# A skip term put into the PSUM bank ahead of the products of a Mamba-2 chunk

## The chip, the cores and the metric

The kernel runs on one NeuronCore of a Trainium2 chip, all in fp32. The metric is the device time of one execution in microseconds; the time of the kernel before is the median of three runs. One further execution was profiled, and every duration below is from that one.

## What is computed

The input is one sequence of 2048 tokens and 1024 channels. It is layer-normalised, and the output is the input plus two branches of the normalised `xn`: a Mamba-2 mixer (64 heads of 64 channels in 8 groups, state size 128), and a dense layer with a mixture of eight low-rank adapters. Of the mixer, this is what matters here:

```python
xBC = silu(conv(hbc))                        # four taps along the tokens
state = state * dA_t + dtx_t * B_t           # for each token t
y_t   = state . C_t
y  = y + x * D                               # the skip: one D per head
yg = y.reshape(L, 8, 512)                    # eight groups of 512 channels
yn = yg * rsqrt(mean(yg * yg) + eps) * norm_weight
out = (yn * silu(gate)) @ out_proj_w.T
```

## The kernel before

Everything is kept with channels on the partitions and tokens along the free dimension. The large products (input projection, base layer, output projection) are done by Strassen-Winograd schemes: seven products in place of eight, with sums formed on VectorE and GpSimd. Over the first 2700 us or so the input projection and the scan run interleaved, and the output projection follows.

**The stream of products.** `pair` makes seven products of one pair of weight tiles, each of four matmuls with 512 moving columns (eight records in the trace, for a fp32 matmul is issued as two instructions). It is a generator, and `products(n, side)` takes n products from it and puts the steps of `side` between them. A product's bank comes from the pool `ps_proj` (four banks). Its sums are taken out by VectorE (L478, L482, and L531 in `stored`) or by ScalarE (L474, L529), and for the gate ScalarE then applies Silu (L533).

**The scan.** The sequence is cut into two segments of 1024 tokens, a segment into eight groups and two halves of 512: 32 blocks. A block has four chunks of 128 tokens, and each chunk has a slot in the main loop, some 128 slots in all. In a slot the loop issues, in this order: one product; `norm_mean` of the block before (first slot only); `scan_b` of this chunk; the first step of `scan_a` for the next chunk (the decay scan, L688); a product; the second step of `scan_a`; two products; its third step; and what products are left. The convolution of the next block (`conv`, L640, L646, L653) is spread over the second and third slots of a block, `norm_squares` over the fourth slot, and `norm_gate` over the first slot of the next block.

- `scan_a`, second step: one product C.B and a transpose of B into the bank `aux` (`ps_cb`), copied out by ScalarE as `cbm` (L698) and `bt` (L700); VectorE then multiplies the decays by `cbm` (L702). Third step: four transposes of x into `aux` (`ps_xt`), and sixteen ScalarE copies with a scale: `xdt` (L713) and `xdd` (L721).
- `scan_b`: for each of eight heads a product of `xdt` with the decayed C.B, 128 tokens wide and 64 output partitions, into the bank `y` of the pool `ps_one` (`ps_y`); four products of the state with C into the bank `e` (`ps_e`); on VectorE `ecp * ps_e` (L763) and the sum with `ps_y` into the SBUF tile `y` (L764), or a plain copy (L761) where there is no state yet; then the new state in the bank `st` (L766 to L778).
- `norm_squares`: for each of four tiles, `x * D + y` on VectorE, written over x (L797); squares of it on ScalarE, written over `y` (L802); two sums on VectorE (L804, L805). `norm_mean` adds over channels on TensorE (`ps_nv`, in the bank `aux`) and takes the root on ScalarE (L813).

Each pool `ps_one` bank has one buffer, so whoever writes it next waits until its last reader is done. TensorE's instructions, and the scaled copies of `scan_a`, keep the order of the program (`keep_in_program_order`); the order of the other instructions in each engine's queue is chosen by the framework when it builds the kernel, and is then fixed. Each engine takes its queue in order.

Of the kernel before, what the change touches and what calls it, by code (L numbers as in the profile page):

```python
# [8 lines left out]
F32 = mybir.dt.float32  # L9
AF = mybir.ActivationFunctionType  # L10
ALU = mybir.AluOpType
# [16 lines left out]
P = 128  # L28
TS = 1024
NS = L // TS  # L30
TB = 512
Q = 128
# [10 lines left out]
def mamba_lora_kernel(  # L43
# [17 lines left out]
    nc = tc.nc  # L61
# [9 lines left out]
    ps_one = ctx.enter_context(tc.tile_pool(name="ps_one", bufs=1, space=bass.MemoryType.PSUM))  # L71
    scan_ctx = ExitStack()
    p1 = scan_ctx.enter_context(tc.tile_pool(name="p1", bufs=1))
# [4 lines left out]
    def mm(*args, **kw):  # L78
        tc.keep_in_program_order(nc.tensor.matmul(*args, **kw))  # L79

    def gp(s, *args):

        ins = nc.gpsimd.tensor_tensor(*args)  # L83
        if s:
            tc.keep_in_program_order(ins)

    def transpose(out, in_):
        tc.keep_in_program_order(nc.tensor.transpose(out, in_, ident))  # L88
# [4 lines left out]
    ident = const.tile([P, P], F32, name="ident")  # L93
# [45 lines left out]
    dsk = p1.tile([P, INNER // P], F32, name="dsk")  # L139
# [465 lines left out]
    def steps(gen, n):  # L605

        return [lambda: next(gen, None) for _ in range(n)]


    xbc_of = {}  # L610
# [46 lines left out]
    mid_of = {}  # L657
    decay_of = {}

    def load_decays(s, g, half, c):  # L660

        da_d, run_d = decay_d[s, half * NQ + c]
        n = f"{s}_{g}_{half}_{c}"
        dab = p2.tile([P, HG * Q], F32, tag="dab", name=f"dab_{n}")
        nc.sync.dma_start(
            dab,
            da_d[g * HG : (g + 1) * HG, :].rearrange("h t -> (h t)").unsqueeze(0)
            .to_broadcast([P, HG * Q]),
        )
        ecp = p2.tile([P, 4, Q], F32, tag="ecp", name=f"ecp_{n}")  # L670
        runs = run_d[g * HG : (g + 1) * HG, :].rearrange("(j a) t -> a j t", a=2)
        for a in range(2):
            nc.sync.dma_start(
                ecp[a * HP : (a + 1) * HP],
                runs[a].unsqueeze(0).to_broadcast([HP, 4, Q]),
            )
        decay_of[s, g, half, c] = dab.rearrange("p (h t) -> p h t", t=Q), ecp

    def scan_a(s, g, half, c):

        key = s, g, half, c
        n = f"{s}_{g}_{half}_{c}"
        dab, ecp = decay_of.pop(key)
        hs = slice(g * HG, (g + 1) * HG)
        cs = slice(c * Q, (c + 1) * Q)

        es = p1.tile([P, HG, Q], F32, tag="es", name=f"es_{n}")
        nc.vector.tensor_tensor_scan(  # L688
            es.rearrange("p h t -> p (h t)"), dab.rearrange("p h t -> p (h t)"), here, 0.0,
            ALU.mult, ALU.add,  # L690
        )
        yield
        xg, bc = xbc_of[s, g, half]
        psm = ps_one.tile([P, 2, Q], F32, tag="aux", name=f"ps_cb_{n}")
        mm(psm[:, 0, :], bc[:, 0, cs], bc[:, 1, cs], start=True, stop=True)
        transpose(psm[:, 1, :], bc[:, 0, cs])
        cbm = p2.tile([P, Q], F32, tag="cbm", name=f"cbm_{n}")
        nc.scalar.copy(cbm, psm[:, 0, :])  # L698
        bt = p2.tile([P, Q], F32, tag="bt", name=f"bt_{n}")
        nc.scalar.copy(bt, psm[:, 1, :])  # L700
        ms = dab
        nc.vector.tensor_tensor(  # L702
            ms, es, cbm.unsqueeze(1).to_broadcast([P, HG, Q]), ALU.mult
        )
        yield
        pst = ps_one.tile([P, 4, Q], F32, tag="aux", name=f"ps_xt_{n}")
        for j in range(4):
            transpose(pst[:, j, :], xg[:, j, cs])
        xdt = p2.tile([P, HG, HP], F32, tag="xdt", name=f"xdt_{n}")
        x_t = pst.rearrange("p j (a q) -> p (j a) q", q=HP)  # L710
        for h in range(HG):
            at = g * HG + h
            ins = nc.scalar.activation(  # L713
                xdt[:, h, :], x_t[:, h, :], AF.Copy,
                scale=dt_of[s][:, half * NQ + c, at : at + 1],
            )
            tc.keep_in_program_order(ins)

        xdd = p1.tile([P, HG, HP], F32, tag="xdd", name=f"xdd_{n}")
        for h in range(HG):  # L720
            ins = nc.scalar.activation(  # L721
                xdd[:, h, :], xdt[:, h, :], AF.Copy, scale=es[:, h, Q - 1 : Q]
            )
            tc.keep_in_program_order(ins)
        mid_of[key] = ms, ecp, bt, xdt, xdd
        yield

    y_of = {}
    state_of = {}

    def scan_b(s, g, half, c):
        xg, bc = xbc_of[s, g, half]
        ms, ecp, bt, xdt, xdd = mid_of.pop((s, g, half, c))
        n = f"{s}_{g}_{half}_{c}"
        hs = slice(g * HG, (g + 1) * HG)
        cs = slice(c * Q, (c + 1) * Q)
        begins, ends = half == 0 and c == 0, half == 1 and c == NQ - 1
        first = s == 0 and begins
        last = s == NS - 1 and ends
        if c == 0:  # L740
            y_of[s, g, half] = p1.tile([P, 4, TB], F32, tag="y", name=f"y_{n}")
        if begins:
            state_of[g] = p2.tile([P, HG * HP], F32, tag="state", name=f"state_{s}_{g}")
            if s:
                nc.sync.dma_start(state_of[g], kept["state", g])
        sv = state_of[g]
        y = y_of[s, g, half]
        psy = ps_one.tile([P, 4, Q], F32, tag="y", name=f"ps_y_{n}")
        pse = None if first else ps_one.tile([P, 4, Q], F32, tag="e", name=f"ps_e_{n}")
        for h in range(HG):  # L750
            a, j = h % 2, h // 2
            o = slice(a * HP, (a + 1) * HP)
            mm(psy[o, j, :], xdt[:, h, :], ms[:, h, :], start=True, stop=True)
        if not first:
            for j in range(4):
                mm(
                    pse[:, j, :], sv[:, j * P : (j + 1) * P], bc[:, 1, cs],
                    start=True, stop=True,
                )
        if first:  # L760
            nc.vector.tensor_copy(y[:, :, cs], psy)  # L761
        else:
            nc.vector.tensor_tensor(ecp, ecp, pse, ALU.mult)  # L763
            nc.vector.tensor_tensor(y[:, :, cs], ecp, psy, ALU.add)  # L764
        if last:
            return  # L766
        pss = ps_one.tile([P, HG * HP], F32, tag="st", name=f"ps_st_{n}")
        mm(pss, bt, xdd.rearrange("p h q -> p (h q)"), start=True, stop=True)
        if first:
            nc.scalar.copy(sv, pss)  # L770
        else:
            s3 = sv.rearrange("p (h q) -> p h q", q=HP)
            gp(
                s, s3, s3,
                tot_of[s][:, half * NQ + c, hs].unsqueeze(2).to_broadcast([P, HG, HP]),
                ALU.mult,
            )
            nc.vector.tensor_tensor(sv, sv, pss, ALU.add)  # L778
        if ends:
            kept["state", g] = dram.tile([P, HG * HP], F32, tag=f"st_{g}", name=f"st_{g}")  # L780
            nc.sync.dma_start(kept["state", g], sv)
# [10 lines left out]

    def norm_squares(s, g, half):

        y, xg = y_of[s, g, half], xbc_of[s, g, half][0]
        for j in range(4):
            nc.vector.scalar_tensor_tensor(  # L797
                xg[:, j, :], xg[:, j, :], dsk[:, 4 * g + j : 4 * g + j + 1], y[:, j, :],
                ALU.mult, ALU.add,
            )  # L800
            if j % 2:
                nc.scalar.activation(y[:, j - 1 : j + 1, :], xg[:, j - 1 : j + 1, :], AF.Square)  # L802
                yield
        nc.vector.tensor_tensor(y[:, 0:2, :], y[:, 0:2, :], y[:, 2:4, :], ALU.add)  # L804
        nc.vector.tensor_tensor(y[:, 0, :], y[:, 0, :], y[:, 1, :], ALU.add)  # L805
        yield
# [90 lines left out]
    here = p1.tile([P, HG * Q], F32, name="here")  # L897
# [58 lines left out]
    load_decays(*blocks[0], 0)  # L956
    products(14, steps(conv(*blocks[0]), 7))
    load_decays(*blocks[0], 1)
    for _ in scan_a(*blocks[0], 0):
        pass  # L960
    done = 7 * PRE
# [16 lines left out]
    for b, blk in enumerate(blocks):  # L978
        s, g, half = blk
# [15 lines left out]
        for c in range(NQ):  # L995
            slot += 1
            n = target(slot) - done
# [30 lines left out]
            if c == 0 and prev:  # L1028
                norm_mean(*prev)
            scan_b(*blk, c)  # L1030
            if b == 14 and c:
                next(left_sums)
# [31 lines left out]
            if after == 0 and c == 3:  # L1064
                sm = lp.tile([P, 2, NSM], F32, tag="sm", name=f"sm_{piece[0]}_{piece[1]}")
                ps = ps_one.tile([P, 2, NSM], F32, tag="st", name=f"ps_sm_{piece[1]}")
# [40 lines left out]
    for _ in passes[1:]:  # L1107
        o = places[-1]
# [125 lines left out]
    for t, (s, p) in enumerate(passes):  # L1234
        last = t + 1 == len(passes)
        for u, i in enumerate(units):
# [89 lines left out]
            for n, j in enumerate(inner):  # L1326
                w = w_ready.pop(0)
                ps = {1: pa, 2: pa, 6: px, 7: px, 4: px, 5: py, 3: py}[j]
                for q in range(2):
                    for k in range(KH):  # L1330
                        mm(
                            ps[:, q, :], w[:, q, k, :], ops[j][:, k, :],
                            start=(n < 3 and q + k == 0), stop=(k == KH - 1), skip_group_check=True,
# [69 lines left out]
```

## Time and profile before

| what | value |
|---|---|
| median of three runs | 3449.89 us (3449.82 to 3451.58) |
| the profiled execution | 3453.59 us, of it 3451.8 us from the first to the last instruction |
| TensorE busy | 3409.2 us (99%), 12818 matmul instructions |
| VectorE busy | 2501.2 us (72%), 2861 instructions |
| ScalarE busy | 1164.7 us (34%), 3182 instructions |
| GpSimd busy | 696.1 us (20%), 443 instructions |
| mean granted TensorE clock | 0.997 |

The page gives busy time by engine, the chain of work that ended last, and groups of instructions by line; "L797" is line 797 of the kernel before, and `xg<-xg,dsk,y` is what is written and what is read. Matmuls all have line 79 (the helper `mm`) or 88 (`transpose`), so they are told apart by the tile. A matmul's duration in the trace overlaps with the next one's: a product of eight records takes 3.43 us from its start to the next one's. In the time line, "x8" merges equal neighbours, and what stands in brackets is the idle time before and what ended it.

### The profile page before, as it was taken

What the parts mean: (1) busy time and instruction counts of PE and PEld (TensorE: products, weight loads), DVE (VectorE), ACT (ScalarE), POOL (GpSimd) and SP (SyncE); (2) the same over time, 40 slices, a digit from 0 to 9 for tenths busy, and PEclk for the clock granted to TensorE, in tenths of its full rate; (3) what the DMA queues carried; (4) which work ended last, traced back from release to release, by engine and by line L of the source; (5) the groups of instructions that cost most, each with busy time, mean ns of one, the idle gap of its engine ahead of it and who ended that gap; (6) DMA issues with size and microseconds to landing.
All of it is one profiled execution on the core that took longest, in us unless ns stands there. A gap on an engine that the chain in (4) does not pass through costs nothing.

```text
span 3451.8 us, 38274 instructions
## 1 busy us (share of the span) xinstructions
PE 3409.2 (99%) x12818; PEld 1992.3 (58%) x12818; DVE 2501.2 (72%) x2861; ACT 1164.7 (34%) x3182; POOL 696.1 (20%) x443
## 2 busy tenths in 40 slices
PE   9999999999999999999999999999999999999999
PEld 7444544544545544454455445444444588888888
DVE  7548877877977877777787877777775466566665
ACT  2234453444444443444445444444442100000000
POOL 3122223222222211322223232222321000000000
PEclk9999999999999999999999999999999999999999
DMA  6546655655666676887778887777778687586654
GB/s 235 186 166 197 205 191 186 211 187 197 203 200 204 205 254 219 291 256 231 236 242 260 236 258 244 245 237 236 228 239 267 243 277 242 196 299 188 214 164 146
DMA packets 530324, 769.83 MB, mean 223 GB/s; under 512 B 35152, under 2 KB 264656, under 8 KB 527440
## 3 DMA queue, kind: packets, MB, share of 16 engines
q1 hardware_dynamic: 530128, 767.39, 68.7%
q8 instruction: 102, 1.67, 0.2%
q14 instruction: 94, 0.77, 0.1%
HBM read 516.64 MB, written 250.61 MB: 222 GB/s over the span
## 4 chain that ended last, share of the span: by engine, by line
PE 84%; DVE 9%; issue 3%; ACT 2%; DMA 1%; POOL 0%; SPq 0%; DVEq 0%; ACTq 0%; POOLq 0%
PE ps_x_x L79 12%; PE ps_x_w L79 8%; PE ps_a_x L79 8%; PE ps_y_x L79 8%; PE ps_x_g L79 7%; PE ps_a_w L79 6%; PE ps_y_w L79 6%; PE ps_y_g L79 5%; PE ps_a_g L79 4%; PE ps_y L79 3%; PE ps_e L79 3%; PE ps_st L79 2%; PE ps_x_b L79 2%; DVE xg L646 2%; PE ps_a_b L79 2%
## 5 line engine op out<-in xcount | busy, mean ns | idle before, releaser
L83 POOL TENSOR_TENSOR state<-state,tot 128x512 f32<-128x512 f32 x112 | 153.7, 1373 | 1326.0 <-PE ps_e L79 1199.8
L688 DVE TENSOR_TENSOR_SCAN es<-dab,here 128x1024 f32<-128x1024 f32 x128 | 304.6, 2380 | 83.4 <-ACT xdd L721 81.8
L646 DVE SCALAR_TENSOR_TENSOR xg<-rawx,cw,xg 128x512 f32<-128x512 f32 x384 | 339.2, 933 | 18.7 <-ACT xg L640 18.0
L79 PE MATMUL ps_x_w<-t,w 128*128 128x256 f32 x1344 | 303.8, 379 | 0.0
L713 ACT ACTIVATE xdt<-ps_xt,dt 128x64 f32<-128x64 f32 x1024 | 223.8, 333 | 209.7 <-PE ps_xt L88 209.7
L79 PEld LDWEIGHTS ps_x_w<-t,w 128*128 128x128 f32 x1344 | 255.4, 190 | 41.5 <-issue 7.7
L721 ACT ACTIVATE xdd<-xdt,es 128x64 f32<-128x64 f32 x1024 | 261.9, 388 | 0.0
L1340 ACT COPY s<-ps_a_w 128x512 f32<-128x512 f32 x28 | 16.4, 586 | 636.0 <-PE ps_a_w L79 555.5
L83 POOL TENSOR_TENSOR wo<-wo 128x512 f32<-128x512 f32 (+1 forms) x112 | 213.4, 1906 | 6.8
L79 PE MATMUL ps_a_w<-q,w 128*128 128x256 f32 x896 | 202.5, 379 | 0.0
L702 DVE TENSOR_TENSOR dab<-es,cbm 128x1024 f32<-128x1024 f32 x128 | 180.1, 1407 | 29.6 <-ACT cbm L698 29.6
L79 PEld LDWEIGHTS ps_a_w<-q,w 128*128 128x128 f32 x896 | 170.2, 190 | 23.6 <-issue 0.5
L79 PEld LDWEIGHTS ps_y<-dab,xdt 128*64 128x64 f32 x2048 | 114.6, 139 | 105.1 <-ACT xdd L721 38.7
L79 PE MATMUL ps_x_x<-op_again,s_x 128*128 128x512 f32 x384 | 172.7, 592 | 0.0
L79 PE MATMUL ps_y_x<-op_again,s_x 128*128 128x512 f32 x384 | 172.7, 592 | 0.0
L79 PE MATMUL ps_a_x<-op_again,a_x 128*128 128x512 f32 x384 | 172.7, 592 | 0.0
L79 PE MATMUL ps_x_x<-op,s_x 128*128 128x512 f32 x368 | 165.5, 592 | 0.0
L79 PE MATMUL ps_y_x<-op,s_x 128*128 128x512 f32 x368 | 165.5, 592 | 0.0
L79 PE MATMUL ps_a_x<-op,a_x 128*128 128x512 f32 x368 | 165.4, 592 | 0.0
L79 PE MATMUL ps_y<-dab,xdt 128*64 128x128 f32 x2048 | 146.6, 284 | 7.8 <-ACT xdt L713 7.8
L531 DVE TENSOR_TENSOR ev<-ps_x_x,s_x 128x512 f32<-128x512 f32 x94 | 64.5, 687 | 120.5 <-PE ps_x_x L79 116.1
L646 DVE SCALAR_TENSOR_TENSOR bc<-rawb,cw,bc 128x512 f32<-128x512 f32 x192 | 145.7, 790 | 1.9 <-ACT bc L640 1.0
(236 smaller groups left out, 6118.6 us busy)
## 6 DMA issues: line engine op xcount, KB each, us to landing
w<-w SPq DMA_DIRECT2D x196, 512.0 KB, 3.7
dab<-da_d SPq DMA_DIRECT2D x128, 512.0 KB, 5.5
raw<-ev SPq DMA_DIRECT2D x192, 256.0 KB, 3.3
a_x<-in_w_in_dram SPq DMA_DIRECT2D x168, 256.0 KB, 4.2
w<-wo SPq DMA_DIRECT2D x96, 448.0 KB, 4.3
ecp<-run_d SPq DMA_DIRECT2D x256, 128.0 KB, 4.0
gate<-ev SPq DMA_DIRECT2D x128, 256.0 KB, 3.9
sg<-gate SPq DMA_DIRECT2D x32, 1024.0 KB, 7.8
```

Source lines behind the costliest of these rows:

```text
L79: tc.keep_in_program_order(nc.tensor.matmul(*args, **kw))
L83: ins = nc.gpsimd.tensor_tensor(*args)
L531: nc.vector.tensor_tensor(e, ps, add, alu)
L646: nc.vector.scalar_tensor_tensor(dst[:, i, :], raw[:, i, k : k + TB], cw[:, ti, k : k + 1], dst[:, i, :], ALU.mult, ALU.add,)
L688: nc.vector.tensor_tensor_scan(es.rearrange("p h t -> p (h t)"), dab.rearrange("p h t -> p (h t)"), here, 0.0, ALU.mult, ALU.add,)
L702: nc.vector.tensor_tensor(ms, es, cbm.unsqueeze(1).to_broadcast([P, HG, Q]), ALU.mult)
L713: ins = nc.scalar.activation(xdt[:, h, :], x_t[:, h, :], AF.Copy, scale=dt_of[s][:, half * NQ + c, at : at + 1],)
L721: ins = nc.scalar.activation(xdd[:, h, :], xdt[:, h, :], AF.Copy, scale=es[:, h, Q - 1 : Q])
L1340: nc.scalar.copy(s1, pa)
```

## The change

The skip term is no longer added by VectorE after the scan. For each chunk ScalarE writes `x * D` of its 128 tokens into the bank `y`, in four instructions, and the eight products of `scan_b` then add to what lies there (`start=False`). `scan_a` takes the bank, in its second step, after the copies `cbm` and `bt`; before, `scan_b` took it. The one VectorE sum that reads the bank (L764, or the copy L761) now gives the finished value and writes it over x. The four `x * D + y` of a block are gone, and the tile `y` now only holds the squares. Ahead of the first chunk one matmul with 512 columns is added, that writes the bank with `start=True`[...].

```diff
@@ scan_a, second step, after the copies cbm and bt
+        psy = ps_one.tile([P, 4, Q], F32, tag="y", name=f"ps_y_{n}")
+        for j in range(4):
+            at = 4 * g + j
+            nc.scalar.activation(
+                psy[:, j, :], xg[:, j, cs], AF.Copy, scale=dsk[:, at : at + 1]
+            )
@@ scan_b
-        if c == 0:
-            y_of[s, g, half] = p1.tile([P, 4, TB], F32, tag="y", name=f"y_{n}")
...
-        psy = ps_one.tile([P, 4, Q], F32, tag="y", name=f"ps_y_{n}")
...
-            mm(psy[o, j, :], xdt[:, h, :], ms[:, h, :], start=True, stop=True)
+            mm(
+                psy[o, j, :], xdt[:, h, :], ms[:, h, :], start=False, stop=True,
+                skip_group_check=True,
+            )
...
         if first:
-            nc.vector.tensor_copy(y[:, :, cs], psy)
+            nc.vector.tensor_copy(xg[:, :, cs], psy)
         else:
             nc.vector.tensor_tensor(ecp, ecp, pse, ALU.mult)
-            nc.vector.tensor_tensor(y[:, :, cs], ecp, psy, ALU.add)
+            nc.vector.tensor_tensor(xg[:, :, cs], ecp, psy, ALU.add)
@@ norm_squares
-        y, xg = y_of[s, g, half], xbc_of[s, g, half][0]
-        for j in range(4):
-            nc.vector.scalar_tensor_tensor(
-                xg[:, j, :], xg[:, j, :], dsk[:, 4 * g + j : 4 * g + j + 1], y[:, j, :],
-                ALU.mult, ALU.add,
-            )
-            if j % 2:
-                nc.scalar.activation(y[:, j - 1 : j + 1, :], xg[:, j - 1 : j + 1, :], AF.Square)
-                yield
+        xg = xbc_of[s, g, half][0]
+        y = y_of[s, g, half] = p1.tile([P, 4, TB], F32, tag="y", name=f"sq_{s}_{g}_{half}")
+        for j in (0, 2):
+            nc.scalar.activation(y[:, j : j + 2, :], xg[:, j : j + 2, :], AF.Square)
+            yield
@@ ahead of the first chunk
+    ps = ps_one.tile([P, 4 * Q], F32, tag="y", name="ps_clear")
+    mm(ps, ident, here[:, 0 : 4 * Q], start=True, stop=True)
```

More of the change, by code (lines that the diff above doesn't have):

```diff
@@ L724, in scan_a @@
             tc.keep_in_program_order(ins)
-        mid_of[key] = ms, ecp, bt, xdt, xdd
+        mid_of[key] = ms, ecp, bt, xdt, xdd, psy
         yield
@@ L732, in scan_b @@
         xg, bc = xbc_of[s, g, half]
-        ms, ecp, bt, xdt, xdd = mid_of.pop((s, g, half, c))
+        ms, ecp, bt, xdt, xdd, psy = mid_of.pop((s, g, half, c))
         n = f"{s}_{g}_{half}_{c}"
@@ L746, in scan_b @@
         sv = state_of[g]
-        y = y_of[s, g, half]
-        psy = ps_one.tile([P, 4, Q], F32, tag="y", name=f"ps_y_{n}")
         pse = None if first else ps_one.tile([P, 4, Q], F32, tag="e", name=f"ps_e_{n}")
```

## The prediction

> **What bounds the kernel now.** I read the busy times first, then the chain, then the gaps of TensorE one by one, then what lies around each.
>
> ```profile
> span 3451.8 us, 38274 instructions
> PE 3409.2 (99%) x12818; PEld 1992.3 (58%) x12818; DVE 2501.2 (72%) x2861; ACT 1164.7 (34%) x3182; POOL 696.1 (20%) x443
> PE 84%; DVE 9%; issue 3%; ACT 2%; DMA 1%; POOL 0%; SPq 0%; DVEq 0%; ACTq 0%; POOLq 0%
> ```
>
> TensorE is the bound. It idles 3451.8 - 3409.2 = 42.6 us, some 9 of them at the very start and end (4.4 before the first matmul, about 4.9 after the last). The chain's 9% for VectorE is no 300 us to be had: where TensorE waits 2 us, the chain goes back through all the VectorE work that made it late. What the change can win is the idle time that is VectorE's doing, and no more. So: who makes TensorE wait?
>
> ```profile
> PE ps_nv L79 <- ACT xdt L713: 10.5, 4, 3.3
> PE ps_y L79 <- ACT xdt L713: 7.8, 5, 4.6
> PE ps_x_x L79 <- DVE ev L531: 2.8, 3, 1.3
> PE ps_x_g L79 <- DVE ev L531: 2.5, 5, 0.9
> ```
>
> (Columns: us in total, times, longest.) The first row names ScalarE's `xdt`, but ScalarE is 34% busy. The time line of one of the four, engine by engine, shows what held it:
>
> ```profile
> 1557.20 5.42 DVE L797 SCALAR_TENSOR_TENSOR xg<-xg,dsk,y 128x512 f32<-128x512 f32 x4
> ...
> 1566.68 3.52 DVE L646 SCALAR_TENSOR_TENSOR bc<-rawb,cw,bc 128x512 f32<-128x512 f32 x5
> 1570.11 0.68 DVE L531 TENSOR_TENSOR ev<-ps_x_g,s_g 128x512 f32<-128x512 f32 x1
> ```
> ```profile
> 1570.83 0.63 ACT L533 ACTIVATE ev<-ev 128x512 f32<-128x512 f32 x1 [6.46 <-DVE ev L531]
> 1571.37 1.73 ACT L713 ACTIVATE xdt<-ps_xt,dt 128x64 f32<-128x64 f32 x8
> ```
> ```profile
> 1573.15 1.12 PE L79 MATMUL ps_nv<-y,ones 128*128 128x512 f32 x2 [3.27 <-ACT xdt L713]
> ```
>
> VectorE runs without a pause from L797 to L531; ScalarE's Silu (L533) waits for L531, `xdt` stands behind it in ScalarE's queue, and TensorE waits for `xdt`. The four skip sums took 5.42 us here.
>
> [...] For `xdd` (64 columns, pointer scale) [...] the trace has eight in 2.04 us with the last lasting 0.388, so 236 ns. [...] no trace of before shows an engine-written seed. [...]
>
> **The change, part by part.**
>
> *VectorE, removed.*
>
> ```profile
> L797 DVE SCALAR_TENSOR_TENSOR xg<-xg,dsk,y 128x512 f32<-128x512 f32 x128 | 119.6, 990 | 0.0
> ACT y L802 <- DVE xg L797: 109.9, 43, 8.6
> ```
>
> 119.6 us of VectorE work go, 3.7 us per block (990 ns on average, 745 in the median; the long ones run beside GpSimd's sums). Most of it lay beside running products and is worth nothing. I went through every gap of TensorE. Those with an L797 in the backlog of VectorE that made it: 0.26 at 1417, 3.27 at 1570, 0.28 and 2.10 at 2158 and 2166, 0.37 and 2.45 at 2314 and 2318, 2.69 at 2469: 11.4 us. Three were followed by a slower clock: from `ps_nv` to the next product took 5.54, 5.52 and 5.52 us, and 3.94 after the gap at 2318 where the clock stayed up, so 1.6 us each, 4.8 us: 16.2 us in all. Three more gaps, at 701, 951 and 1199, end the router's long chain of small VectorE steps. VectorE works without a pause from L797 up to them, but the chain's first step (L311) needs ScalarE's copy of the router sums, which ended 0.86, 0.20 and 0.62 us before it began; more than that can't be won: **1.7 us**. What is late next: at 1570, VectorE 5.4 us earlier puts L531 at about 1566.7 (then bound by its own product and five `bc` steps), Silu ends at 1567.4, `xdt` at about 1569.5, and TensorE comes at 1569.9. So that gap closes with 0.4 us to spare; the three others have more. The other gaps stay: 4.58 us at 447 plus 1.8 of clock (9% of 20 us) come from the same chain, but there VectorE paused for 1.2 us between L797 and it; two of 0.9 at 726 and 1224 wait for ScalarE's copy of the decays; 0.5 to 1.3 us at 1607, 1973, 2126, 2349 and 2506 come from the `xg` convolution in the third slot.
>
> *ScalarE, added.* Four writes of 128 columns per chunk. [...] from the narrower price of `cbm` (261 ns, the next starting 160 ns later) 0.75 us. I take 1.3[...]. Where do they lie? Behind `bt`, with ScalarE idle until the transposes come; this row alone is 210 us:
>
> ```profile
> ACT xdt L713 <- PE ps_xt L88: 209.7, 48, 6.9
> L764 DVE TENSOR_TENSOR y<-ecp,ps_y 128x512 f32<-128x512 f32 x120 | 80.9, 674 | 2.2
> ```
>
> Cost 0. If that cover is gone in a slot, `xdt` is 1.3 us later, and TensorE has a product of 3.4 us between `ps_xt` and what needs `xdt`.
>
> *The new wait.* ScalarE's first write waits until L764 (or L761) of the chunk before has read the bank. I compared the end of all 120 L764 with the end of the `bt` that follows: L764 is done earlier in 116 (median 3.0 us earlier); in four it is later, by 0.16, 0.35, 0.93 and 2.14 us, and there `xdt` starts 4.8 to 14 us after it. Behind the waiting write stand the evacuations L474/L529, Silu and `xdt`; all come later than that. Cost 0, at worst 2 us in one slot.
>
> *TensorE.* `ps_y` already waits for `xdt`, which stands behind the writes in ScalarE's queue, so it gets no later wait. Adding in place of overwriting: a fp32 matmul is two records, [...] and both go at the same pace (16 in 1.02 us). Cost 0. The clearing matmul: two records of 512 columns at 0.43 us, **0.9 us**, on the bound, as nothing hides it. The square waits for L764 in place of L797, so comes earlier. No DMA is added or moved.
>
> *Sum.* 16.2 + 1.7 - 0.9 = 17.0 us off the profiled 3453.6 us: 3436.6. That execution was 3.7 us above the median, so against the median: 3449.9 - 17.0 = 3432.9, say 3433.
>
> **The rivals.**
>
> *A larger gain.* The queues' orders are made anew, and a lighter VectorE might also let the gaps of the `xg` convolution (4.4 us) and the one at 447 (6.4 with its clock) go. For it: VectorE is 72% busy and late by 1 us or less in most of them. Against it: L797 isn't in the slots concerned. With 9 of those us: 3424. Chance 0.16.
>
> *Given back by the order.* The writes aren't kept in program order, and on ScalarE they are ready before `cbm`. Or a step slips in front of an evacuation elsewhere, and new gaps of 1 to 3 us come in some five to eight slots: 13 us back, 3446. Nothing in the profile shows the new order, so I give it 0.19.
>
> *Slower.* The writes stand ahead of `cbm` in ScalarE's queue. Then `cbm` comes up to 1.3 us later, VectorE stands still before L702 for as long, and in the third slot of each block, where five gaps show that VectorE has no slack, the evacuations behind it make TensorE wait. 31 such slots x 1.3 = 40 us, less 17: 3473. It decides where L764 ends less than 1.3 us before `ps_cb` is ready. Against it: in those slots L764 ended 1.9, 2.1 and 3.0 us ahead of `cbm` (2117, 1598, 2343), though only 0.6 at 1969. [...] Chance 0.09.
>
> *It doesn't do what it says*: if products overwrote the seed, times would be those of the forecast; no case of its own.
>
> **How the numbers follow.** The forecast, 3433 (3427 to 3440), has 0.56, the larger gain 0.16, given back 0.19, slower 0.09. A measurement of this kernel can tell about 0.2%, or 7 us: faster means under 3443, slower over 3456.8. Faster: 0.56 + 0.16 + a fifth of "given back" = 0.75; slower 0.09 and a little of "given back", 0.10; the same 0.15. The range leaves out the slower case and the far ends of the two next: 3419 to 3449.
>
> **What would show it.** Right: no row of L797; gaps of `ps_nv` behind `xdt` gone, or under 1 us in all; clock 1.00 around them; L802 waiting little; the gap at 447 still there; `ps_y` at 1.02 us per chunk; the four writes at about 1.3 us behind `bt`, ended ahead of `xdt`. Wrong: TensorE idle still over 35 us, new gaps with `cbm` or the writes behind them, `ps_y` slower than 1.02 us per chunk.

## The result, and the profile after

The kernel after takes 3439.63 us (median of six, 3437.45 to 3442.42) against 3451.36 (six, 3449.82 to 3453.5) for the kernel before: a ratio of 0.9965, with a 95% interval of 0.9952 to 0.9978, so 12 us off, between 8 and 17. The two profiled executions lie 16.1 us apart (3453.59 and 3437.5), with spans of 3451.8 and 3435.7. They flatter the change: a gap of TensorE at 141 us, ahead of the scan, cost 3.1 us less after (the gap itself 3.97 against 1.99, the rest in the product behind it, which took 6.34 us before and 5.21 after where the next ones take 3.43; the granted clock in the 20 us behind the gap was 0.86 and 0.91). In the profiles of the experiments below it is between 2.4 and 4.1 us whatever the edit.

The page's busy times and the engines' shares of the chain, after:

```profile
span 3435.7 us, 38674 instructions
PE 3404.6 (99%) x12820; PEld 1989.8 (58%) x12820; DVE 2410.5 (70%) x2733; ACT 1338.9 (39%) x3694; POOL 697.2 (20%) x443
PE 87%; DVE 8%; issue 2%; DMA 2%; ACT 2%; SPq 0%; DVEq 0%; ACTq 0%
```

TensorE idles 31.1 us, where it idled 42.6. It is also busy 4.6 us less, in spite of the clearing matmul, since fewer of its matmuls run at the slow clock: in the 20 us after the gaps at 1570, 2166 and 2469 the granted clock was 0.91, and at the same three places of the run after it is 1.00. Idle time fell by 11.5 and busy time by 4.6, together 16.1. The waits of TensorE in the kernel after (us in total, times, longest) say which idle time went:

```profile
PE ps_y L79 <- ACT xdt L720: 6.9, 5, 4.6
...
PE ps_x_x L79 <- DVE ev L531: 4.1, 4, 1.3
PE ps_x_g L79 <- DVE ev L531: 3.3, 6, 1.1
...
PE ps_nv L79 <- ACT xdt L720: 0.6, 1, 0.6
```

The row of `ps_nv` fell from 10.5 to 0.6 us; the two rows behind L531 grew from 5.3 to 7.4. The same slot that the prediction took apart (product, `ps_nv`, `xdt`), now about 5 us earlier in the run, on VectorE, ScalarE and TensorE:

```profile
1554.72 4.78 DVE L646 SCALAR_TENSOR_TENSOR bc<-rawb,cw,bc 128x512 f32<-128x512 f32 x3
...
1562.90 2.19 DVE L646 SCALAR_TENSOR_TENSOR bc<-rawb,cw,bc 128x512 f32<-128x512 f32 x3
1565.01 0.68 DVE L531 TENSOR_TENSOR ev<-ps_x_g,s_g 128x512 f32<-128x512 f32 x1
```
```profile
1556.15 1.56 ACT L705 ACTIVATE ps_y<-xg,dsk 128x128 f32<-128x128 f32 x4
1557.65 0.26 ACT L698 COPY cbm<-ps_cb 128x128 f32<-128x128 f32 x1
...
1565.72 0.63 ACT L533 ACTIVATE ev<-ev 128x512 f32<-128x512 f32 x1 [4.99 <-DVE ev L531]
1566.26 1.73 ACT L720 ACTIVATE xdt<-ps_xt,dt 128x64 f32<-128x64 f32 x8
```
```profile
1563.81 3.60 PE L79 MATMUL ps_y_g<-op_again,s_g 128*128 128x512 f32 x8
1568.04 1.12 PE L79 MATMUL ps_nv<-sq,ones 128*128 128x512 f32 x2 [0.63 <-ACT xdt L720]
```

L531 starts 1.2 us after the start of the last product ahead of `ps_nv` (1563.81), where it was 3.8 us before. The gap is 0.63, from 3.27. It isn't quite closed because three convolution steps moved into the place of L797 and took 1.59 us each there, 4.78 together; the three further down take 0.73 each. And the writes stand ahead of `cbm`, not behind `bt`.

Two groups of the page before, and three of the page after (busy us, mean ns of one | idle before it, and who ended that):

```profile
L702 DVE TENSOR_TENSOR dab<-es,cbm 128x1024 f32<-128x1024 f32 x128 | 180.1, 1407 | 29.6 <-ACT cbm L698 29.6
L646 DVE SCALAR_TENSOR_TENSOR bc<-rawb,cw,bc 128x512 f32<-128x512 f32 x192 | 145.7, 790 | 1.9 <-ACT bc L640 1.0
```

```profile
L705 ACT ACTIVATE ps_y<-xg,dsk 128x128 f32<-128x128 f32 x512 | 190.2, 371 | 222.5 <-DVE xg L770 192.9
L709 DVE TENSOR_TENSOR dab<-es,cbm 128x1024 f32<-128x1024 f32 x128 | 177.6, 1388 | 39.3 <-ACT cbm L698 39.0
L646 DVE SCALAR_TENSOR_TENSOR bc<-rawb,cw,bc 128x512 f32<-128x512 f32 x192 | 163.8, 885 | 1.9 <-ACT bc L640 1.3
```

L709 is the former L702. The `bc` steps rose from 145.7 us to 163.8: 18.1 us of what L797 gave up went there, and 9.1 more to the two sums of squares (L806 and L807, formerly L804 and L805: 73.9 against 64.8). So VectorE's busy time fell by 90.7 us, not by 119.6.

Where the 16.1 us came in, from the start of each chunk's `ps_y` before and after:

| place | us gained |
|---|---|
| start, gap at 141 and its clock, less the clearing matmul | +2.05 |
| clock after the gap at 447 (4.58 and 4.57 us) | -0.95 |
| router, gaps at 630, 701, 951, 1199 | +1.37 |
| fourth slots of blocks 16, 24, 26, 28 (gap and clock) | +14.6 |
| gap at 2126 (0.53 to 1.23) | -0.70 |
| the rest | -0.3 |

Of the two rows on top I count only the 0.86 us of clearing as the change's: the gap at 141 lies ahead of the scan, and the gap at 447 is as long as before. The other rows come to 15.0 us; less the clearing that is some 14 us, and it lies within the 8 to 17 of the medians.

### The profile page after: what moved, and what is told of

It reads as the page before. It is cut to its first block, busy times and chain, and to the rows that moved or that the text cites. A ratio compares the mean times of both kernels' runs of the same rounds, so it can differ in the third digit from the quotient of the medians.

```text
span 3435.7 us, 38674 instructions
## 1 busy us (share of the span) xinstructions
PE 3404.6 (99%) x12820; PEld 1989.8 (58%) x12820; DVE 2410.5 (70%) x2733; ACT 1338.9 (39%) x3694; POOL 697.2 (20%) x443
## 4 chain that ended last, share of the span: by engine, by line
PE 87%; DVE 8%; issue 2%; DMA 2%; ACT 2%; SPq 0%; DVEq 0%; ACTq 0%
PE ps_x_x L79 12%; PE ps_x_w L79 8%; PE ps_a_x L79 8%; PE ps_y_x L79 8%; PE ps_x_g L79 8%; PE ps_y_w L79 6%; PE ps_a_w L79 6%; PE ps_y_g L79 5%; PE ps_a_g L79 5%; PE ps_y L79 3%; PE ps_e L79 3%; PE ps_st L79 3%; PE ps_x_b L79 2%; DVE xg L646 2%; PE ps_a_b L79 2%
## 5 line engine op out<-in xcount | busy, mean ns | idle before, releaser
L705 ACT ACTIVATE ps_y<-xg,dsk 128x128 f32<-128x128 f32 x512 | 190.2, 371 | 222.5 <-DVE xg L770 192.9
L1345 ACT COPY s<-ps_a_w 128x512 f32<-128x512 f32 x28 | 16.4, 585 | 636.2 <-PE ps_a_w L79 555.6
L709 DVE TENSOR_TENSOR dab<-es,cbm 128x1024 f32<-128x1024 f32 x128 | 177.6, 1388 | 39.3 <-ACT cbm L698 39.0
L646 DVE SCALAR_TENSOR_TENSOR bc<-rawb,cw,bc 128x512 f32<-128x512 f32 x192 | 163.8, 885 | 1.9 <-ACT bc L640 1.3
L531 DVE TENSOR_TENSOR ev<-ps_x_x,s_x 128x512 f32<-128x512 f32 x94 | 64.4, 686 | 129.3 <-PE ps_x_x L79 124.2
```

The costliest lines, as they stand in the source:

```text
L531: nc.vector.tensor_tensor(e, ps, add, alu)
L646: nc.vector.scalar_tensor_tensor(dst[:, i, :], raw[:, i, k : k + TB], cw[:, ti, k : k + 1], dst[:, i, :], ALU.mult, ALU.add,)
L705: nc.scalar.activation(psy[:, j, :], xg[:, j, cs], AF.Copy, scale=dsk[:, at : at + 1])
L709: nc.vector.tensor_tensor(ms, es, cbm.unsqueeze(1).to_broadcast([P, HG, Q]), ALU.mult)
L1345: nc.scalar.copy(s1, pa)
```

## Experiments

Each kernel is compared with runs of the kernel before from its own batch. The first batch has the three kernels with VectorE work put back and the one without the skip, with 3452.37 us for the kernel before. The second has the kernel with the writes too, the one with them behind `bt`, and the first two moves of GpSimd's sums, with 3453.93. The third has the other three moves and the kernel without the gate's Silu, with 3454.54.

**The removed VectorE work, put back.** My theory: the gain is VectorE's lateness in four fourth slots and nothing else. Three kernels put four steps of L797's form per block back (two inputs in SBUF, here the same tile twice), ahead of the squares: in all blocks, in the four blocks whose fourth slot had a gap, and in the other 28. The diff is that of the second; the first has no condition, the third the opposite one.

```diff
@@ after, norm_squares, ahead of the squares
+        for j in range(4):
+            if (16 * s + 2 * g + half) in (16, 24, 26, 28):
+                nc.vector.scalar_tensor_tensor(
+                    xg[:, j, :], xg[:, j, :], 1.0, xg[:, j, :], ALU.mult, ALU.max
+                )
```

> The changed kernel, with four VectorE operations of 128x512 put back into the fourth slot of every block, in the place of the skip sums (the larger of x and 1*x, so x stays as it is). Theory (the gain is the VectorE time of the fourth slot): the gain of the change is lost, the time is within 4 us of the kernel before, and the four gaps of TensorE before ps_nv (11 us with their slow clock 15 us) are back. Rival (the gain comes from another order of the queues, or from the bank being taken earlier): it stays 10 us or more under the kernel before.

> The same four VectorE operations, in four blocks only: 16, 24, 26 and 28, whose fourth slots ended in a gap of TensorE before the change. Theory: 128 operations in 32 blocks or 16 operations in these four are the same to the time; nearly all of the gain is lost, it is within 5 us of the kernel before. Rival (VectorE work counts everywhere, some 0.4 us per block): an eighth of the gain is lost, 1 to 2 us, so it is 10 us under the kernel before.

> The same four VectorE operations in the 28 other blocks, and not in 16, 24, 26 and 28. Theory: they cost nothing but the 0.9 us that the router's chain won at three places; the time is within 3 us of the changed kernel, some 9 to 12 us under the kernel before. Rival (VectorE work counts everywhere): seven eighths of the gain are lost, within 3 us of the kernel before.

In all: 3454.07 us, ratio 1.0004 (0.9996 to 1.0012). In the four: 3451.55, 1.0000 (0.9991 to 1.0008). In the other 28: 3440.10, 0.9961 (0.9948 to 0.9975). The wait of `ps_nv` with all of it back, and then with the four blocks alone:

```profile
PE ps_nv L79 <- ACT xdt L720: 10.2, 4, 3.4
```
```profile
PE ps_nv L79 <- ACT xdt L720: 10.2, 4, 3.4
```

Sixteen instructions out of 128, 21.4 us of VectorE, take the whole gain back; the other 112, with 68.6 us more VectorE busy time than after (2479.1), take nothing that could be measured. The theory held. The sixteen took 21.4 us, but VectorE's busy time rose by only 7.5 (2410.5 to 2418.0), since their neighbours became shorter: the `bc` steps fell from 163.8 us to 153.0.

These kernels also showed something that I had wrong: the router's gap at 701 is 0.7 us in all three profiles (1.06 before), in the first and the third with VectorE's work back ahead of it. Its small gain isn't from L797.

**The rest of the change, alone.** First the kernel before with the writes, the clearing matmul and the adding products, and L797 kept. That is the diff of the change without its part in `norm_squares`, and with the sum (L764) written to `y` as before. Then the kernel after without the writes, the clearing and the skip; the bank is taken in `scan_b` again:

```diff
@@ after, scan_a, second step
-        psy = ps_one.tile([P, 4, Q], F32, tag="y", name=f"ps_y_{n}")
-        for j in range(4):
-            at = 4 * g + j
-            nc.scalar.activation(
-                psy[:, j, :], xg[:, j, cs], AF.Copy, scale=dsk[:, at : at + 1]
-            )
...
@@ scan_b
...
-            mm(
-                psy[o, j, :], xdt[:, h, :], ms[:, h, :], start=False, stop=True,
-                skip_group_check=True,
-            )
+            mm(psy[o, j, :], xdt[:, h, :], ms[:, h, :], start=True, stop=True)
@@ ahead of the first chunk
-    mm(ps, ident, here[:, 0 : 4 * Q], start=True, stop=True)
```

> The kernel before with only the new part added: the four writes by ScalarE into the bank, the clearing matmul, and products that add; the skip sums on VectorE stay, so the skip term counts twice in the result. Theory (the new part is hidden, the gain is the removed VectorE work): the time of the kernel before plus 0 to 3 us. Rival (the bank and the writes change something by themselves): 5 us or more away from the kernel before, on either side.

> The changed kernel without the skip term at all: no writes by ScalarE, no clearing matmul, the products overwrite the bank as before. x times D is left out of the result. It shows what the writes, the wait and the clearing cost together. Theory (the writes are hidden; only the clearing matmul is on the bound): 1 us under the changed kernel, at most 3, so 11 to 15 us under the kernel before. Rival (the writes stand in ScalarE's queue ahead of cbm and give part of the gain back): 5 us or more under the changed kernel, 17 or more under the kernel before.

The first took 3454.41, ratio 1.0002 (0.9994 to 1.0010), with the old gaps:

```profile
PE ps_nv L79 <- ACT xdt L720: 10.5, 4, 3.3
```

The second took 3439.14, 0.9958 (0.9946 to 0.9971), half a microsecond from the kernel after by the medians (0.7 x 10^-3 by the ratios, with intervals that overlap). So 512 writes, 190 us of ScalarE, with their wait and the clearing, cost at most a few microseconds, and the measurement can't tell them from the 0.9 of the clearing or from nothing.

**The order of the writes.** My slower rival was that the writes would stand ahead of `cbm`. They do: in the queue as built, all four stand ahead of it in 86 of 128 chunks, and some ahead and some behind in 14. One kernel keeps the order of the program, for `cbm` as shown and for `bt` and the four writes likewise.

```diff
@@ after, scan_a, second step
-        nc.scalar.copy(cbm, psm[:, 0, :])
+        tc.keep_in_program_order(nc.scalar.copy(cbm, psm[:, 0, :]))
```

> The changed kernel with cbm, bt and the four writes kept in the order of the program on ScalarE: in all 128 chunks the writes stand behind bt, where in the changed kernel they stand ahead of cbm in 86 (and astride in 14). Theory (the order is worth nothing, since VectorE and TensorE have slack there): within 2.5 us of the changed kernel, 9 to 14 us under the kernel before; the gaps of the third slots (about 5.5 us) stay within 1.5 us of that. Rival (cbm behind the writes costs VectorE time in the third slots): 3 to 6 us under the changed kernel, and those gaps fall below 3 us.

3440.08, ratio 0.9965 (0.9952 to 0.9979), as for the kernel after: no worth of the order can be measured. The same two rows of the page:

```profile
L705 ACT ACTIVATE ps_y<-xg,dsk 128x128 f32<-128x128 f32 x512 | 193.2, 377 | 17.0 <-DVE xg L770 4.7
L709 DVE TENSOR_TENSOR dab<-es,cbm 128x1024 f32<-128x1024 f32 x128 | 178.3, 1393 | 33.0 <-ACT cbm L698 33.0
```

In this order ScalarE waits 4.7 us for VectorE's sum in place of 192.9, and `cbm` keeps VectorE waiting 6 us less. Neither shows in the time.

**Through which queue VectorE's lateness reaches TensorE.** In the gap at 1570, `xdt` itself needs only TensorE's transposes; Silu (L533) ahead of it in ScalarE's queue waits for VectorE. The kernel before, with the gate stored as it is, has no L533:

```diff
@@ before, the stream of products
-                        stored(gate_d[g], 2 * q, s, AF.Silu), s == 0,
+                        stored(gate_d[g], 2 * q, s, AF.Copy), s == 0,
```

> The kernel before, with the gate stored as it is: its Silu is left out of the result, and with it the ScalarE step (L533) that waits for VectorE's evacuation and has xdt behind it. VectorE's work is the same. Theory (VectorE's lateness reaches TensorE through ScalarE's queue): the gaps before ps_nv fall from 10.5 us to under 3, the time by 10 to 16 us; the gaps where a product waits for VectorE's evacuation itself stay. Rival (TensorE waits for VectorE's own results, the squares' sum or the bank): the four gaps stay at 2 to 3 us each, the time within 3 us of the kernel before.

3434.33, ratio 0.9944 (0.9932 to 0.9957), with VectorE as busy as before (2497.6 us) and all of L797 in place. That is 20 us off, more than the 10 to 16 expected. No wait of `ps_nv` is left in the trace; by the starts of the chunks, 16.4 of the 19.9 us between the two profiled executions came in at the four slots, and 2.4 ahead of the scan. The slot at 1570 on VectorE, on ScalarE and on TensorE:

```profile
1554.72 5.42 DVE L797 SCALAR_TENSOR_TENSOR xg<-xg,dsk,y 128x512 f32<-128x512 f32 x4
...
1567.63 0.68 DVE L531 TENSOR_TENSOR ev<-ps_x_g,s_g 128x512 f32<-128x512 f32 x1
```
```profile
1563.99 1.75 ACT L713 ACTIVATE xdt<-ps_xt,dt 128x64 f32<-128x64 f32 x8 [2.10 <-PE ps_xt L88]
```
```profile
1567.22 1.02 PE L79 MATMUL ps_nv<-y,ones 128*128 128x512 f32 x2
```

L797 takes its 5.42 us and L531 is as late as before, but `xdt` begins 3.6 us ahead of L531, and `ps_nv` follows the product without a gap. ScalarE has 59 us less to do in this kernel, but its load wasn't what held `xdt` before: it sat idle for 6.46 us ahead of that Silu. The link is the order in ScalarE's queue, not the data.

This also says why only four blocks count. In the kernel before, L797 took 5.2 us or more in the fourth slots of blocks 15, 18, 20, 22 and 30 too, and no gap of `ps_nv` followed. In four of these ScalarE has no L533 between `bt` and `xdt`; in block 22 it has, and `xdt` was done in time.

**Why L797 was slow there: GpSimd's sums, moved.** The prediction noted that the long L797 run beside GpSimd's sums of output weights. Those come in three batches in the second, third and fourth slot of blocks 15 to 30. I first took the convolution's gaps (1607 to 2506) for the third slot's and tried two moves on the kernel after: the third slot's batch to the fourth, as in the diff, and all three to the second.

```diff
@@ main loop, after
-            if 0 <= b - 15 < 16 and c:
-                next(left_sums)
+            if 0 <= b - 15 < 16 and c in (1, 3):
+                next(left_sums)
+                if c == 3:
+                    next(left_sums)
```

> The changed kernel, with GpSimd's second batch of sums for the output weights moved from the third slot of a block to the fourth, behind the third batch's place, now that VectorE has time there. Theory (the remaining gaps of the third slots come from the convolution's VectorE steps, which take 1.4 us in place of 0.74 beside GpSimd's sums): those gaps, 5.2 us in five slots, fall below 2 us; 3 us under the changed kernel, unless the fourth slot becomes late. Rival (they come from the number of VectorE steps): no change, or slower by new gaps in the fourth slot.

> The changed kernel, with all three batches of GpSimd's sums in the second slot of a block, so that the third and fourth slot have none. Theory (VectorE's steps are slow beside GpSimd's sums): the gaps of the third and fourth slots go, some 6 us; the second slot may get some of its own; 3 to 6 us under the changed kernel. Rival: no change, since TensorE's waits are moved to the second slot, whose convolution steps then take 1.4 us each; within 2 us of the changed kernel or slower.

Both are slower even than the kernel before: 3462.51, ratio 1.0029 (1.0018 to 1.0040), and 3527.08, 1.0212 (1.0198 to 1.0226). The aim was wrong, since the gaps are in the second slot, where the first batch runs. But the misses show how far GpSimd's sums stretch VectorE's steps. With two batches in the fourth slot, VectorE at the old place of L797:

```profile
1556.84 6.59 DVE L646 SCALAR_TENSOR_TENSOR bc<-rawb,cw,bc 128x512 f32<-128x512 f32 x3
1563.36 3.09 DVE L806 TENSOR_TENSOR sq<-sq 128x1024 f32<-128x1024 f32 x1
```

A `bc` step costs 2.2 us in place of 0.73, L806 3.09 in place of 1.21, and gaps of 3.05, 4.49, 4.05 and 3.05 us are at the ends of the four fourth slots. With all three in the second, three of its five gaps grow from about 1 us to 8.4, new ones of up to 5.6 come in other blocks, and the clock falls to a mean of 0.989.

Then to the right place: all three batches in the third slot, in the kernel before and in the kernel after; and, in the kernel after, the first batch alone moved to the third slot. The diff is that of the last; the two others have `c == 2` and take all three steps there.

```diff
@@ main loop
-            if 0 <= b - 15 < 16 and c:
-                next(left_sums)
+            if 0 <= b - 15 < 16 and c in (2, 3):
+                next(left_sums)
+                if c == 2:
+                    next(left_sums)
```

> The kernel before, with all three batches of GpSimd's sums of the output weights in the third slot of a block, so that none run beside the skip sums of the fourth slot, nor beside the convolution of the second. Theory (the skip sums made TensorE wait only where GpSimd's sums stretched them from 2.7 to 5.4 us): the four skip sums take 2.7 us in all fourth slots, the four gaps before ps_nv (10.5 us, with the slow clock 15) go without the change, and so do the gaps of the second slots (about 4); 10 to 20 us under the kernel before, unless the third slot gets gaps. Rival (the gaps come from the number of VectorE steps, not from their length beside GpSimd): the four gaps stay at 2 to 3 us each.

> The changed kernel, with the same move of all three batches to the third slot. Theory: the gaps of the second slots (5.4 us) go; 3 to 6 us under the changed kernel, unless the third slot gets gaps. It gains less from the move than the kernel before does, since both take away the same four gaps. Rival: gains add up, 25 us or more under the kernel before.

> The changed kernel, with only the first batch moved, from the second slot to the third; the third batch stays in the fourth. Theory (the remaining gaps of the second slots come from the convolution beside GpSimd's first batch; the two earlier tries did not take it from there): those gaps, 5.4 us in five slots, fall below 1 us; 4 to 6 us under the changed kernel, 16 to 18 under the kernel before. Rival: those gaps stay, within 2 us of the changed kernel.

The kernel before with its sums moved took 3440.56, ratio 0.9962 (0.9950 to 0.9975): about as much as the change itself, with L797 in place. Its four L797 take 2.73 us in the fourth slots (at 1570 they took 5.42), the convolution's gaps in the second slot are gone, and two of the four gaps of `ps_nv` fell to 0.81 and 0.61. The other two did not; they are 3.88 and 4.17:

```profile
PE ps_nv L79 <- ACT xdt L713: 9.5, 4, 4.2
```

In the second of these, ScalarE and VectorE had another wait:

```profile
2451.56 1.52 ACT L640 ACTIVATE bc<-rawb,cb,cw 128x512 f32<-128x512 f32 x2 [11.71 <-DMA rawb<-raw]
...
2453.93 0.24 ACT L698 COPY cbm<-ps_cb 128x128 f32<-128x128 f32 x1
```
```profile
2454.20 1.23 DVE L702 TENSOR_TENSOR dab<-es,cbm 128x1024 f32<-128x1024 f32 x1 [4.23 <-ACT cbm L698]
```

A load of `rawb` lands late, L640 holds `cbm` up in ScalarE's queue, and VectorE stands still for 4.23 us ahead of its backlog. The one at 2305 begins with the same load: ScalarE waits 5.77 us for it ahead of L640. There `cbm` stands ahead of L640, and it is VectorE's `bc` steps that wait for L640, 3.34 us. In the whole run L640 waits 30.1 us for it (13.4 before). In SP's queue, stores of the moved sums (L871) stand ahead of it; that they are what delays it is read from the time line and wasn't tried. So VectorE's longer steps beside GpSimd's sums (at 1570, 5.42 us in place of 2.73) are shown as the cause of two of the four gaps; for the other two the experiment put a new wait in its place. That the time comes out near that of the change is chance: by the starts of the chunks, the two gaps that closed gave 7.7 us, the second slots 7.6, and the two other fourth slots lost 5.8.

With the same move the kernel after took 3437.66, ratio 0.9954 (0.9941 to 0.9968): the two gains hardly add. New gaps of 3.81 and 2.96 us came, and ScalarE waits 25.8 us for `rawb`; which of it makes them wasn't tried. With only the first batch moved it took 3434.44, 0.9946 (0.9933 to 0.9958), the fastest kernel here that leaves nothing out: 20 us under before in its own batch, where 16 to 18 were expected. It is 5 us under the kernel after, which ran in another batch, and the intervals of the two ratios overlap a little, so that these 5 us are likely and not shown. The gaps of the second slot are gone; one of 2.36 at 2301 is new. It waits 25.4 us for `rawb` too, so this wait alone doesn't make a gap.

## Why the prediction was right, and where its steps were not

The forecast was 17.0 us off the profiled time; that fell by 16.1, and the medians by 12 (8 to 17). The time, 3439.6, lies 6.6 us above the forecast and inside its range; 1.5 of these are the kernel before, whose median in the paired runs is 3451.4 and not 3449.9. That 16.1 is so near to 17.0 is in part luck: it has the 3.1 us of the gap at 141 in it, which the forecast didn't count on. What belongs to the change is some 14 us, so the mechanism is right and the forecast 3 us too large, for the reasons in the points on L531, the small gaps, the router and the convolution.

- *VectorE's lateness in four slots, 10.5 us of gaps and 4.8 of clock, 15.3 in all: right.* The gaps fell to 0.6; from `ps_nv` to the next product it is now 3.93 us at 1570, as it was where the clock stayed up. The four places gave 14.6 us. Put back in these four blocks alone, the work takes everything back.
- *"VectorE 5.4 us earlier": wrong in size.* L531 came 2.6 us nearer to its product. The new order put three `bc` steps beside GpSimd's sums, where each took 1.59 us in place of 0.73; in all, 27 us of the 119.6 that L797 gave up came back as longer neighbours. I had priced L797 at what it took, and not seen that part of its length belonged to the place and not to the instruction. A gap of 0.6 us is left where I had 0.4 to spare.
- *The three small gaps of 0.26, 0.28 and 0.37: wrong.* They are 0.27, 0.76 and 0.32. An L797 in the backlog was no proof that the backlog would end sooner without it.
- *The router, 1.7 us: half of it, for another reason.* At 701, 951 and 1199 0.93 us came, and with VectorE's work back ahead of it the gap at 701 is still 0.7. A new order of the queues is the likely cause, and isn't shown; which instruction moved wasn't settled.
- *The convolution's gaps: that they stay held nearly, the place did not.* I had them in the third slot; they are in the second, where GpSimd's first batch runs. They grew by 1.0 us in sum, to 5.4. The two moves that failed rest on this error.
- *ScalarE's writes: cost 0, right.* Four take 1.56 us, not 1.3, which was my estimate. The trace of before gives an estimate as large: eight `xdd` of 64 columns start 236 ns apart, and L338 takes 278 ns for 128 columns and 597 for 512, so 0.83 ns a column, 289 ns a write and 1.3 us for four. In the trace after a write takes 371 ns on average and, in the slot shown, they start 397 ns apart, so there they don't overlap. The count of table loads is the same, 91 in both traces, and none has the writes' line (L705).
- *The wait for the bank: cost 0, right; but the place was wrong.* ScalarE does wait 193 us for L770, since the writes stand ahead of `cbm`; that nothing urgent stands behind them is read from the time, which the order of the program didn't change.
- *TensorE: right.* A record of `ps_y` has a mean of 281 ns (284 before), 16 in 1.02 us from `ps_y` to `ps_e`; the clearing matmul takes 0.86. What the sums would be without it wasn't tried.
- *The slower rival: its mechanism came, its price did not.* The writes stand ahead of `cbm` in most chunks and VectorE's idle time before L709 rose by 9.7 us, against up to 40 us that I had charged to TensorE. With the order of the program the time is the same. Its step "the evacuations behind it make TensorE wait" failed.
- *The larger gain:* the gap at 447 stayed at 4.57. The convolution's gaps can go, but by moving GpSimd's work and not by lightening VectorE.

## What to carry to other kernels

Price removed work by the gaps that it stands in front of, slot by slot: here 16 instructions out of 128 carried the whole gain, and 190 us of new work on an engine that waits cost nothing that could be measured. Before moving work off a late engine, ask through which queue its lateness reaches the bound one, and whether the instruction is slow in itself or in its place; leaving one kind of ScalarE step out, or moving GpSimd's work to another slot, gave about as much as the change or more. A slot that looks free takes only so much: with all of GpSimd's sums in one slot the kernel after became some 85 us slower (an estimate from the two ratios, 1.0212 and 0.9965), and with the first batch alone in another it seems some 5 us faster.

## What I had not expected of the hardware

- VectorE's steps with two SBUF inputs stretch beside GpSimd's sums: L797 from 0.68 us to 1.36 each, `bc` from 0.73 to 1.59 and, with more sums, to 2.2. In the slot of the gap at 1570 it was L797 that took longer before, and `bc` after. L764 of the kernel before, which reads one input from PSUM, takes 0.69 us at most in all 120 places, 41 of which lie beside such sums. GpSimd's sums of 896 columns take about 2.3 us each there (two in 4.57 us before, in 4.58 after). How the sums stretch these steps isn't shown.
- The slower clock after a gap varies. After 3.27, 2.10 and 2.69 us of idle time about 1.6 us were lost, with a granted clock of 0.91 in the 20 us behind the gap, after 2.45 us nothing, with 1.00; and after the gap at 447, of the same length in both traces, the granted clock over the 20 us from the gap's start was 0.91 before and 0.83 after, and up to the start of the next chunk 0.95 us more was lost after. What decides this isn't shown.
